# Layer 0 of a two-layer graph network: a row tile's normalisation, transposes and mask copies issued several units later

**Chip, cores, metric.** One core of one Trainium2 chip. The metric is the device time of one execution in microseconds (us); a kernel's figure is the median of its timed runs. Lower is better.

## The reference, cut to what matters

Two layers over 4096 nodes with 512 features. Layer 0 is a graph attention with four heads and a full 4096 x 4096 0/1 mask, then a residual and a normalisation; layer 1 is a masked attention with eight heads.

```python
support = (inputs @ weight).reshape(N, H, D).transpose(1, 0, 2)     # layer 0, H = 4, D = 128
logits = f1 + f2
w = jnp.where(logits >= 0, logits, SLOPE * logits)
masked = w * adjacency[None]
attn = jax.nn.softmax(jnp.where(masked != 0, masked, NEG), axis=-1) * (masked != 0)
out = jnp.einsum('hij,hjd->hid', attn, support)
out = out + bias + inputs @ proj_w + proj_b
x = _layernorm(x + out)                                             # input of layer 1
# ... layer 1: q, k, v, masked softmax, projection, residual, _layernorm
```

## The kernel before

The program order is the order on each engine: each engine takes its own instructions one after the other (in the prediction's timeline ScalarE's copy at 597.05 starts only after the normalise that waited 5.24 us), and the kernel's author decides by hand where each one stands. A small list named `Later` puts off a piece of work by a number of steps:

```python
class Later:
    def at(self, steps, fn): self.todo.append((self.n + steps, fn))
    def step(self):
        self.n += 1
        due = [fn for n, fn in self.todo if n <= self.n]
        ...
```

Layer 0's attention handles 8 row tiles (a group, W = 1024 rows) at a time, for each of four heads, over 32 column tiles. One (group, head, column tile) is a **unit**: eight matmuls into o_ps. Work of unit n+3 is prepared (`front`) before the matmuls of unit n are issued:

```python
            def front(w, h, j):                       # ... loads cut
                if j % 2 == 0:                        # ScalarE: two masks z, VectorE: az
                    z = wp.tile([P, 2, W], BF16, name="z")
                    ...
                p = wp.tile([P, W], F32, name="p", bufs=LA + 1)      # VectorE; LA = 3
                ...
            for n, (w, h, j) in enumerate(steps):
                if n + LA < len(steps):
                    front(*steps[n + LA])
                ...
                if w + 1 < NW and u % 3 == 0 and u // 3 < NT:        # u = h * NT + j
                    take = transpose_adj(w + 1, u // 3, ps)          # PE: masks of the next group
                for t in range(WT):
                    nc.tensor.matmul(o[t // BK][:, t % BK, :], ...)
                if take:
                    take()                            # ScalarE copies the transposed masks
                if j == NT - 1:
                    finish(w, h, o_t.pop((w, h)))
                later.step()
            later.flush()
```

When a group's last head is done, `finish` plans the **closing** of its eight row tiles, which then runs inside the first units of the next group (for the fourth group there is no next, and it runs alone):

```python
                for t in range(WT):
                    later.at(4 + t, lambda t=t: divide(t))               # ScalarE
                    if h == H0 - 1:
                        later.at(5 + t, lambda t=t: add_base(w, t))      # GpSimd's DMA adds the residual
                        later.at(8 + 3 * t, lambda t=t: close(w, t))

            def close(w, t):
                y = agg_t[w][:, t].rearrange("p h d -> p (h d)")
                mv, rs = moments(y)          # VectorE statistics, GpSimd: + EPS, power -0.5
                nb = small.tile([P, 1], F32, name="nb")                  # GpSimd, two more
                nc.gpsimd.tensor_tensor(nb, mv[:, 0:1], rs, op=ALU.mult)
                nc.gpsimd.tensor_scalar(nb, nb, -1.0, None, op0=ALU.mult)

                def normalise():             # ScalarE, then a store
                    nc.scalar.activation(y, y, AF.Identity, bias=nb, scale=rs)
                    nc.sync.dma_start(x1_d[i], y)
                later.at(2, normalise)
                later.at(4, lambda: turn(y, i))

            def turn(y, i):                  # PE: four transposes into the one bank x_ps
                p = ps.tile([P, KC, P], F32, name="x_ps", bufs=1)
                ...
                later.at(1, lambda: turned(p, i))

            def turned(p, i):                # ScalarE copies the bank out, then a store
                x1T = wp.tile([P, KC, P], F32, name="x1T")
                nc.scalar.activation(x1T, p, AF.Copy)
                nc.sync.dma_start(x1T_d[i // GT]..., x1T)
```

## Time and profile before

| | before |
|---|---|
| median of runs | 3967.98 us (3965.11 to 3968.51) |
| PE busy, whole span | 3799.8 us, 96% |
| layer 0's attention, first matmul to last | 315.84 to 1366.6 us |
| first matmul of layer 1 | 1408.96 us |

In the trace the engines are PE (matmuls), PEld (PE's weight loads), DVE (VectorE), ACT (ScalarE), POOL (GpSimd) and SP (SyncE). The page, the windows, the waits and a piece of timeline are read in the prediction below. One ruler is used all through this text. The mask transposes (at_ps) come every three units in the first three heads of a group, 32 per group. So the distance between two of them on PE's timeline is the time of a known number of units, and can be compared between kernels:

- **closing 1 and 2**: from mask transpose 0 of the second and third group to number 12 (36 units, holding the whole closing of the group before). With PE full this would be 12 x 5.86 + 8 x 0.49 = 74.2 us, from the spacing of mask transposes where PE is full and the time of a tile's x_ps transposes.
- **head 4**: from mask transpose 31 of the second group to the next group's first (35 units, nearly all without masks).
- **last stretch**: from mask transpose 31 of the third group to the last matmul (163 units, holding the third closing).
- **tail**: from the last matmul to layer 1's first. The last matmul's end is the start of the tail's first x_ps transpose minus the wait listed with it.

### The profile page before, as it was taken

What the parts mean: (1) busy time and instruction counts of PE and PEld (TensorE: products, weight loads), DVE (VectorE), ACT (ScalarE), POOL (GpSimd) and SP (SyncE); (2) the same over time, 40 slices, a digit from 0 to 9 for tenths busy, and PEclk for the clock granted to TensorE, in tenths of its full rate; (3) what the DMA queues carried; (4) which work ended last, traced back from release to release, by engine and by line L of the source; (5) the groups of instructions that cost most, each with busy time, mean ns of one, the idle gap of its engine ahead of it and who ended that gap; (6) DMA issues with size and microseconds to landing.
All of it is one profiled execution on the core that took longest, in us unless ns stands there. A gap on an engine that the chain in (4) does not pass through costs nothing. (4 is left out here: it accounts for less than half of the span.)

```text
span 3967.4 us, 51832 instructions
## 1 busy us (share of the span) xinstructions
PE 3799.8 (96%) x20490; PEld 1985.2 (50%) x20490; DVE 2532.6 (64%) x2432; ACT 1855.8 (47%) x2113; POOL 2046.3 (52%) x1211
## 2 busy tenths in 40 slices
PE   7988998999989889989999999999999999999998
PEld 3448998989989734433333333333333333333332
DVE  3447998988989801125666666666666666666665
ACT  1226767767656510024444444444444444444443
POOL 2320012021030100018888888888887888888886
PEclk9998999999999989999999999999999999999999
DMA  6885566656431143242222322322323223223211
GB/s 163 193 199 162 131 195 157 175 161 160 150 109 63 43 148 111 98 146 83 96 83 80 117 83 79 113 88 78 109 74 114 80 88 117 80 77 115 75 63 54
DMA packets 232429, 447.47 MB, mean 113 GB/s; under 512 B 21744, under 2 KB 136688, under 8 KB 225008
## 3 DMA queue, kind: packets, MB, share of 16 engines
q1 hardware_dynamic: 179264, 386.38, 29.4%
q0 software_dynamic: 42432, 51.39, 7.8%
q10 hardware_dynamic: 10480, 6.29, 0.5%
q8 instruction: 163, 2.67, 0.3%
q14 instruction: 90, 0.74, 0.1%
HBM read 372.51 MB, written 100.86 MB: 119 GB/s over the span
## 5 line engine op out<-in xcount | busy, mean ns | idle before, releaser
L959 POOL TENSOR_TENSOR q_sum<-q_sum,p 128x1024 f32<-128x1024 f32 x704 | 1659.0, 2356 | 332.6 <-DVE p L951 287.2
L951 DVE TENSOR_TENSOR p<-s_ps,adjT 128x1024 f32<-128x1024 f32 x896 | 1043.8, 1217 | 686.1 <-ACT s_ps L945 669.1
L945 ACT ACTIVATE s_ps<-s_ps 128x1024 f32<-128x1024 f32 x1024 | 971.1, 1009 | 1004.2 <-PE s_ps L936 1004.1
L796 PE MATMUL o_ps<-sup_t,p 128*128 128x129 f32 x8192 | 966.0, 279 | 42.4 <-DVE p L719 42.4
L936 PE MATMUL s_ps<-q_sb,k_sb 64*128 64x512 f32 x4096 | 981.6, 610 | 16.8 <-issue 10.2
L796 PEld LDWEIGHTS o_ps<-sup_t,p 128*128 128x128 f32 x8192 | 941.5, 194 | 52.2 <-issue 29.6
L969 PE MATMUL o_ps<-p,v_sb 128*64 128x512 f32 x4096 | 956.5, 601 | 0.0
L936 PEld LDWEIGHTS s_ps<-q_sb,k_sb 64*128 64x128 f32 x4096 | 367.6, 187 | 628.4 <-issue 388.4
L719 DVE SCALAR_TENSOR_TENSOR p<-fr_t,dj,az 128x1024 f32<-128x1024 f32 x512 | 635.5, 1280 | 27.7 <-DVE az L715 0.9
L712 ACT ACTIVATE z<-fr_t,f1s 128x1024 bf16<-128x1024 f32 x512 | 555.5, 1141 | 132.8 <-DVE az L715 106.3
L969 PEld LDWEIGHTS o_ps<-p,v_sb 128*64 128x64 f32 x4096 | 263.1, 136 | 649.7 <-issue 621.3
L715 DVE TENSOR_TENSOR az<-adjT,z 128x2048 bf16<-128x2048 bf16 x256 | 311.6, 1217 | 88.4 <-ACT z L712 88.2
L752 POOL DMA_DIRECT2D agg<-base_d x32 | 29.0, 1120 | 443.2 <-ACT agg L740 442.8
L538 POOL DMA_DIRECT2D arow<-in_adj_dram x32 | 30.7, 960 | 402.0 <-PE at_ps L553 402.0
L560 ACT ACTIVATE stage<-at_ps 128x1024 bf16<-128x1024 bf16 x128 | 130.7, 1021 | 206.5 <-PE at_ps L553 200.9
L951 DVE TENSOR_TENSOR p<-s_ps,md 128x1024 f32<-128x1024 f32 x128 | 150.4, 1216 | 94.7 <-ACT s_ps L945 93.4
L886 POOL DMA_DIRECT2D md<-adjT_d x8 | 6.6, 824 | 354.9 <-DMA v_d<-vg 354.6
L840 DVE COPY kg<-k_ps 128x512 f32<-128x512 f32 x32 | 22.1, 692 | 196.2 <-PE k_ps L837 190.1
L980 PE MATMUL sm_ps<-p,ones 128*32 128x512 f32 x1024 | 136.4, 605 | 0.0
L847 ACT ACTIVATE qg<-q_ps 128x512 f32<-128x512 f32 x32 | 19.1, 597 | 237.4 <-PE q_ps L844 237.4
L837 PE MATMUL k_ps<-xT,wk 128*128 128x512 f32 x256 | 118.1, 605 | 12.5 <-DMA xT<-x1T_d 12.5
L661 DVE TENSOR_TENSOR prod<-sup,uv 128x512 f32<-128x512 f32 x64 | 51.7, 807 | 117.6 <-ACT sup L657 117.6
(91 smaller groups left out, 2107.3 us busy)
## 6 DMA issues: line engine op xcount, KB each, us to landing
adjT<-adjT_d SPq DMA_DIRECT2D x64, 1024.0 KB, 7.1
k_sb<-k_d SPq DMA_DIRECT2D x128, 512.0 KB, 3.5
v_sb<-v_d SPq DMA_DIRECT2D x128, 512.0 KB, 3.6
sup_t<-sup_d SPq DMA_DIRECT2D x16, 2064.0 KB, 13.1
arow<-in_adj_dram POOLq DMA_DIRECT2D x32, 1024.0 KB, 12.5
adjT_d<-stage SPq DMA_DIRECT2D x64, 512.0 KB, 5.7
fr_t<-fr_d SPq DMA_DIRECT2D x16, 1024.0 KB, 8.9
sup_d<-sup SPq DMA_DIRECT2D x32, 258.0 KB, 10.9
```

The source lines that it names most:

```text
L560: nc.scalar.activation(s[:, j % 2, :], p.rearrange("p t r -> p (t r)"), AF.Copy)
L712: nc.scalar.activation(z[:, k, :], fr[:, 0, :], AF.Abs, bias=f1s[:, j + k, h:h + 1], scale=BIG)
L715: nc.vector.tensor_tensor(az, adjT[w, j // CJ][:, j % CJ:j % CJ + 2, :], z, op=ALU.min)
L719: nc.vector.scalar_tensor_tensor(p, fr[:, 1, :], dj[:, j, h:h + 1], az_t[w, h, j // 2][:, j % 2, :], op0=ALU.max, op1=ALU.mult)
L796: nc.tensor.matmul(o[t // BK][:, t % BK, :], p[:, t * P:(t + 1) * P], sup_t[w, h][:, j, :], start=(j == 0 and t % BK == 0), stop=(j == NT ...
L837: nc.tensor.matmul(k_ps, w3["wk"][:, c, m * P:(m + 1) * P], xT[:, c, :], start=(c == 0), stop=(c == KC - 1))
L936: nc.tensor.matmul(s[:, e, :], k[r, a:a + P], qt[g, m][r, :], start=True, stop=True)
L945: nc.scalar.activation(s, s, AF.Exp)
L951: nc.vector.tensor_tensor(p, s, mask.to_broadcast([P, HP, G]), op=ALU.mult)
L959: nc.gpsimd.tensor_tensor(q_sum[g, m], q_sum[g, m], p, op=ALU.add)
L969: nc.tensor.matmul(o[r, :], v[:, j % CH, r], p[:, e, :], start=(j == 0), stop=(j == NT - 1))
L980: nc.tensor.matmul(sm_t[g, m][r:r + QD, :], ones[:, 0:QD], pt[g, m, j - 1 + n][:, e, :], start=(j == 3), stop=(j + 6 >= BY_PE))
```

## The change

The intent: put distance between the instruction that needs a result and the one that makes it, so that an engine that takes its work in order doesn't stand in front of a result that is still on its way.

```diff
-                        later.at(8 + 3 * t, lambda t=t: close(w, t))
+                        later.at(8 + 2 * t, lambda t=t: close(w, t))
...
-                later.at(2, normalise)
-                later.at(4, lambda: turn(y, i))
+                later.at(6, normalise)
+                later.at(9, lambda: turn(y, i))
...
-                later.at(1, lambda: turned(p, i))
+                later.at(2, lambda: turned(p, i))
...
                 if take:
-                    take()
+                    later.at(2, take)
```

The cut rest gathers the statistics and the four GpSimd operations into one helper, `normal_factors`, also used by the last layer, with the same operations in the same order. `take` is called outside a step, so `at(2, take)` means the end of the next unit.

More of the change, by code (lines that the diff above doesn't have):

```diff
@@ L508, in on_all_partitions, with normal_factors @@
         return bass.AP(tensor=src.tensor, offset=src.offset, ap=[[0, P], [1, n]])
-    def moments(y):
+    def normal_factors(y):
         st = small.tile([P, 6], F32, name="bn_st")
@@ L518, in moments @@
         nc.gpsimd.tensor_tensor(rs, ve, minus_half, op=ALU.pow)
-        return mv, rs
-    def layernorm(dst, y):
-        mv, rs = moments(y)
-        nc.vector.tensor_scalar(dst, y, mv[:, 0:1], rs, op0=ALU.subtract, op1=ALU.mult)
+        nb = small.tile([P, 1], F32, name="bn_nb")
+        nc.gpsimd.tensor_tensor(nb, mv[:, 0:1], rs, op=ALU.mult)
+        nc.gpsimd.tensor_scalar(nb, nb, -1.0, None, op0=ALU.mult)
+        return rs, nb
     with tc.tile_pool(name="l0", bufs=1) as l0, \
@@ L757, in close @@
                 y = agg_t[w][:, t].rearrange("p h d -> p (h d)")
-                mv, rs = moments(y)
-                nb = small.tile([P, 1], F32, name="nb")
-                nc.gpsimd.tensor_tensor(nb, mv[:, 0:1], rs, op=ALU.mult)
-                nc.gpsimd.tensor_scalar(nb, nb, -1.0, None, op0=ALU.mult)
+                rs, nb = normal_factors(y)
                 def normalise():
@@ L1016, in close1 @@
                 nc.vector.tensor_tensor(y, y, s, op=ALU.add)
-                mv, rs = moments(y)
-                nb = small.tile([P, 1], F32, name="nb")
-                nc.gpsimd.tensor_tensor(nb, mv[:, 0:1], rs, op=ALU.mult)
-                nc.gpsimd.tensor_scalar(nb, nb, -1.0, None, op0=ALU.mult)
+                rs, nb = normal_factors(y)
                 def normalise():
```

## The prediction

> **What bounds the kernel now.** I read the page first, then busy time by windows, then the waits of one window, then its timeline.
>
> ```profile
> PE 3799.8 (96%) x20490; PEld 1985.2 (50%) x20490; DVE 2532.6 (64%) x2432; ACT 1855.8 (47%) x2113; POOL 2046.3 (52%) x1211
> PE   7988998999989889989999999999999999999998
> ```
>
> PE is the engine to feed, and 96% leaves 168 us without a matmul in the whole kernel. The 9s with 8s between them are layer 0's attention, slices 3 to 13. It runs four groups of eight row tiles; a group takes 128 units (four heads of 32), a unit being eight matmuls. The group's normalisation and transposes ("closing") run inside the first units of the next group. Windows (us from the start, PE, PEld, DVE, ACT, POOL busy, granted clock, DMA share, GB/s):
>
> ```profile
> 570.00:660.00 90.00, 76.02 (x670) 73.62 (x669) 69.08 (x75) 59.36 (x73) 35.28 (x43) 0.96 0.61 138
> 660.00:840.00 180.00, 180.00 (x1674) 178.95 (x1673) 172.37 (x160) 125.36 (x137) 5.29 (x6) 1.00 0.59 178
> 840.00:930.00 90.00, 74.75 (x667) 72.00 (x667) 68.92 (x74) 59.38 (x73) 34.99 (x42) 0.98 0.62 141
> 930.00:1097.00 167.00, 167.00 (x1548) 165.89 (x1547) 159.51 (x144) 117.96 (x129) 2.63 (x3) 1.00 0.52 160
> 1097.00:1185.00 88.00, 72.91 (x599) 70.66 (x599) 72.23 (x76) 45.59 (x56) 33.02 (x40) 0.96 0.38 100
> 1366.00:1409.00 43.00, 9.59 (x39) 6.22 (x37) 7.67 (x20) 12.77 (x24) 20.60 (x44) 0.55 0.87 230
> ```
>
> Between closings PE is full at clock 1.00. In the three closings it loses 14 to 15 us each and the clock dips. The last window is the fourth closing, with no matmuls left to hide it. Waits from 570 to 650 (us, times, longest):
>
> ```profile
> ACT agg L764 <- POOL nb L761: 28.3, 5, 6.0
> DVE az L715 <- ACT z L712: 14.1, 4, 3.6
> PE x_ps L772 <- ACT x1T L777: 10.1, 4, 3.1
> PE o_ps L796 <- DVE p L719: 2.9, 3, 1.1
> ```
>
> These are one chain read from the top: POOL delivers the factors late, ACT stands before its normalise, and behind it in ACT's order stand the copy that frees PE's only transpose bank and the masks z that DVE needs. The timeline (start, duration, engine, operation):
>
> ```profile
> 591.14 0.18 DVE L514 BATCH_NORM_AGGREGATE bn_mv<-bn_st 128x2 f32<-128x6 f32 x1
> ...
> 591.42 1.15 POOL L516 TENSOR_SCALAR bn_ve<-bn_mv 128x1 f32<-128x1 f32 x1 [3.75 <-DVE bn_mv L514]
> 592.66 1.41 POOL L518 TENSOR_TENSOR bn_rs<-bn_ve,minus_half 128x1 f32<-128x1 f32 x1
> 594.15 0.92 POOL L760 TENSOR_TENSOR nb<-bn_mv,bn_rs 128x1 f32<-128x1 f32 x1
> 595.15 1.15 POOL L761 TENSOR_SCALAR nb<-nb 128x1 f32<-128x1 f32 x1
> ...
> 596.33 0.81 ACT L764 ACTIVATE agg<-agg,nb,bn_rs 128x512 f32<-128x512 f32 x1 [5.24 <-POOL nb L761]
> 597.05 0.57 ACT L777 ACTIVATE x1T<-x_ps 128x512 f32<-128x512 f32 x1
> 597.68 0.66 PE L772 MATMUL x_ps<-ident,agg 128*128 128x128 f32 x4 [3.08 <-ACT x1T L777]
> 598.17 2.88 PE L796 MATMUL o_ps<-sup_t,p 128*128 128x129 f32 x16
> ```
>
> The wait ends 5.2 us after the statistics. It arises because tile t's copy and tile t+1's normalise fall into the same unit (13+3t), the normalise first. The matmuls after it take 2.88 us instead of the usual 1.95: the clock from 599.0 to 601.7 was 0.50.
>
> **What the Trainium skill says.** "GPSIMD Engine Reference", Specifications: its SBUF interfaces are shared with VectorE and contend with DVE instructions in a two-port mode or with two SBUF inputs. The trace agrees: the four POOL operations take 1.15, 1.41, 0.92 and 1.15 us beside a running DVE and 0.22, 0.57, 0.19 and 0.24 at 599.1 when DVE stands. "TensorE: Matmul & The Clock Gate", Part 1, says an idle window of about 3.4 us brings half clock; here 3.08 us (with 1.14 shortly before) did. "Perfetto Trace Analysis", Identifying the Most-Contended Engine: consistent bubbles can mean too few buffers; with one x_ps bank the bubbles are consistent, but the bank is held by a late copy, so order may cure it. "DMA: Bandwidth & Descriptors", Anatomy of one DMA, gives about 2 us fixed cost; the store of x1T lands after a median of 6.2 us, so load decides here.
>
> **The change part by part.** Closings start every 2 units instead of 3. The normalise comes 6 units after the statistics (was 2), the transposes after 9 (was 4), the copy out of x_ps 2 units after them (was 1); a mask transpose is copied at the end of the next unit (was the same). The number of matmuls, activations, bytes and POOL operations is the same; the last layer's close only gets a shared helper, with its order kept. So nothing is saved in work; only waits can go.
>
> (a) What is to be had, first two closings. Mask transposes start every 5.86 us (three units) where PE is full. Eight such groups, 24 units, with eight sets of x_ps transposes at 0.49 us of issue, should take 8 x 5.86 + 8 x 0.49 = 50.8 us. From the mask transpose at 580.99 to that at 650.88 they take 69.9: 19.1 lost, 14.0 as listed waits and the rest as slow clock. Second closing, 850.69 to 926.43, nine groups: 75.7 against 56.7, also 19.1.
> (b) Third closing. No mask transposes; DVE sets the pace at 3.72 us for two units (az 1.23, two p 2.48). A tile's statistics add about 0.82 to 0.85. From 1111.47 to 1185.21 there are 28 units: 14 x 3.72 + 8 x 0.85 = 58.9 us expected, 73.7 taken: 14.8 lost.
> Sum 19.1 + 19.1 + 14.8 = 53.0 us.
>
> (c) Does the new order fit? In units: the copy of tile t stands at 19+2t, its neighbours' normalises at 18+2t and 20+2t, the next transposes at 19+2t. The normalise before it, of tile t+2, had its statistics at 12+2t, six units or some 13 us before. Per two units PE needs 2 x 1.805 + 0.30 (masks) + 0.49 = 4.4 us; DVE 3.72 + 0.85 = 4.57; ACT start to start 2.09 (two z) + 0.72 + 0.48 + 0.60 (masks) = 3.9. DVE falls back 0.17 x 8 = 1.4 us in a closing, and its four p buffers allow a lead of three units, over 5 us. POOL needs 4 to 4.9 us per tile beside DVE, and the base DMAs (0.92 each) and an adjacency load lie between the early tiles, so it lags by some 4 to 5 us: factors about 9 us after the statistics, four units. ACT runs up to four units ahead, so it may still wait there, but then keeps about two units before anything is needed. The next transposes wait for a copy that has two units (4 us) to take 0.6. I charge 1 us per closing: gain 50.
>
> (d) The tail after the last matmul has no matmuls to delay behind, so later issue there is pure order. POOL has eight closes at 1.5 us and eight base DMAs at 0.92, ending near 1389 in both orders. But the first copy now stands after the third normalise (about 1381, was 1378.4), and x1T has two buffers, so each copy waits for a store two tiles back, at the 4.5 to 8.3 us these stores took. Worked through, the last copy ends 0 to 4 us later than now (1400.4). I charge 2 us.
>
> Net 50 - 2 = 48 us, 1.2%: 3968 - 48 = 3920.
>
> **The rivals.**
> 1. POOL takes the place of the removed wait. For: 4.9 us per tile against closings every 4.57, and its queue holds the base DMAs too. Against: it is short of rate only by little and over eight tiles; two units of slack remain. If its lag doubled, half the 53 us would stay: 3943.
> 2. Copies wait for the x1T stores. For: in the first two closings these stores landed after 9.1 and 9.3 us (median), and two tiles now pass in about 9.0 us, so each pair may slip by about 1 us. Against: three slips of 1 us stay under the two units of slack; in the third closing stores landed in 2.8. If the slack were used up: some 10 us lost, 3930.
> 3. The order is neutral because DVE is the bound anyway. In the stretches between closings PE and DVE are almost level, so DVE caps the gain; but DVE itself was kept idle 14.1 us by ACT in the first closing. That it caps all: 3955 at the worst, and unlikely.
> 4. More gain than counted, by a shorter tail: its 43 us are mostly POOL and DMA latency, which the change doesn't shorten. A few us at best: 3912.
>
> **Range and chances.** The mechanism is listed wait by wait, and nothing in work is added, so the sign is fairly sure. Two per cent is 79 us, more than all the waits of the three closings and half of the tail together. Runs of before lie within 3.4 us. Predicted 3921 (one more us for rivals), range 3911 to 3939; faster by over 2%: 0.02, within 2%: 0.97, slower: 0.01.
>
> **What would show each step.** Right: in the closings' windows PE over 98% busy at clock 1.00; PE's waits for x1T gone before the tail (23 us or more now) and its waits for p down to the first 29.4; mask transposes near 50.8 us for eight groups; ACT still waiting for nb in short pieces, without PE waiting after. The tail 43 to 47 us. Wrong: PE still waiting for x1T with ACT behind nb (rival 1) or behind x1T stores (rival 2); PE waiting for p or at_ps in the closings, which would mean that ACT's lead was miscounted; or a tail longer than 50 us.

## The result

| | before | changed |
|---|---|---|
| median | 3968.12 us (3965.11 to 3968.51, 4 runs) | 3913.89 us (3910.23 to 3914.50, 4 runs) |
| ratio | | 0.9863, 95% interval 0.9846 to 0.9880 |
| closing 1 | 93.5 | 76.4 |
| closing 2 | 93.5 | 78.6 |
| head 4 | 64.5 | 63.0 |
| last stretch | 328.3 | 311.8 |
| tail | 42.3 | 42.2 |
| layer 1's first matmul at | 1408.96 | 1356.10 |

A ratio is the mean time of one kernel's runs over that of the other's in the same rounds, so it is not quite the ratio of the medians. By the criterion of 2% the two count as the same; the interval shows a real gain of 1.4%, 54 us.

The ruler itself, on PE's timeline (start, duration, engine and line, operation, count, wait in brackets). Before:

```profile
580.99 0.61 PE L553 MATMUL at_ps<-ident_b,arow 128*128 128x128 bf16 x8
588.82 0.61 PE L553 MATMUL at_ps<-ident_b,arow 128*128 128x128 bf16 x8 [0.54 <-ACT stage L560]
600.85 1.06 PE L553 MATMUL at_ps<-ident_b,arow 128*128 128x128 bf16 x8
607.90 0.61 PE L553 MATMUL at_ps<-ident_b,arow 128*128 128x128 bf16 x8
```

The changed kernel, the same three distances:

```profile
579.13 0.61 PE L553 MATMUL at_ps<-ident_b,arow 128*128 128x128 bf16 x8
585.23 0.61 PE L553 MATMUL at_ps<-ident_b,arow 128*128 128x128 bf16 x8
...
592.49 0.61 PE L553 MATMUL at_ps<-ident_b,arow 128*128 128x128 bf16 x8
599.25 0.61 PE L553 MATMUL at_ps<-ident_b,arow 128*128 128x128 bf16 x8
```

Where three units took 7.8, 12.0 and 7.1 us they now take 6.1, 7.3 and 6.8. The windows of the changed kernel (columns as in the prediction):

```profile
570.00:630.00 60.00, 58.82 (x550) 57.83 (x550) 58.14 (x60) 51.02 (x61) 36.16 (x41) 1.00 0.79 184
820.00:880.00 60.00, 57.18 (x529) 55.54 (x528) 57.73 (x60) 48.26 (x59) 35.96 (x41) 1.00 0.77 177
1060.00:1140.00 80.00, 75.38 (x651) 73.08 (x650) 76.92 (x87) 53.16 (x63) 35.93 (x40) 1.00 0.53 154
```

The closings are shorter, and the clock stays at 1.00 in all three, where it was 0.96 to 0.98. PE is not quite full in the second and third: in the third DVE is the busiest (76.9 of 80). Waits of the changed kernel from 570 to 650 (us, times, longest):

```profile
ACT agg L761 <- POOL bn_nb L522: 3.9, 4, 1.9
ACT x1T L774 <- DMA x1T_d<-x1T: 3.2, 2, 1.8
...
PE o_ps L793 <- DVE p L719: 1.2, 3, 0.7
```

ScalarE still stands before a normalise now and then, but 3.9 us instead of 28.3, and PE doesn't wait for the copy at all there. A new small wait has come: the copy waits for an older store (x1T_d). The same two waits over all of layer 0's attention and the tail, 330 to 1440, before:

```profile
ACT agg L764 <- POOL nb L761: 103.5, 19, 8.4
PE x_ps L772 <- ACT x1T L777: 43.9, 19, 3.8
```

The changed kernel:

```profile
ACT agg L761 <- POOL bn_nb L522: 28.8, 20, 5.4
PE x_ps L769 <- ACT x1T L774: 16.4, 9, 6.6
```

Of PE's waits for the copy, 13.4 us lie in the tail before and 15.0 in the changed kernel.

**Where the 52.9 us to layer 1's first matmul came from.** Start of the attention 0.2, first group 1.7, closing 1 17.2, the rest of the second group 1.8 (head 4 1.5), closing 2 14.9, the rest of the third group's heads with masks 0.6, last stretch 16.5, tail 0.1: together 53.0, the difference being rounding. From there to the end the two traces differ by another 2.3 us in a layer whose order is the same; over all twelve traces that stretch scatters between 2555.5 and 2559.9 us without pattern, so it is taken as noise.

### The profile page after: what moved, and what is told of

Its sections match the earlier page's. It is cut to its first block, busy times and chain, and to the rows that moved or that the text cites. A ratio compares the mean times of both kernels' runs of the same rounds, so it can differ in the third digit from the quotient of the medians.

```text
span 3912.2 us, 51842 instructions
## 1 busy us (share of the span) xinstructions
PE 3780.8 (97%) x20490; PEld 1971.1 (50%) x20490; DVE 2536.0 (65%) x2432; ACT 1858.0 (47%) x2113; POOL 2055.2 (53%) x1211
## 5 line engine op out<-in xcount | busy, mean ns | idle before, releaser
L933 PE MATMUL s_ps<-q_sb,k_sb 64*128 64x512 f32 x4096 | 980.9, 610 | 16.4 <-issue 10.1
L793 PE MATMUL o_ps<-sup_t,p 128*128 128x129 f32 x8192 | 951.6, 277 | 37.9 <-DVE p L719 37.8
L793 PEld LDWEIGHTS o_ps<-sup_t,p 128*128 128x128 f32 x8192 | 929.7, 192 | 46.1 <-issue 29.4
L715 DVE TENSOR_TENSOR az<-adjT,z 128x2048 bf16<-128x2048 bf16 x256 | 311.7, 1218 | 26.6 <-ACT z L712 26.5
```

The source lines that it names most:

```text
L715: nc.vector.tensor_tensor(az, adjT[w, j // CJ][:, j % CJ:j % CJ + 2, :], z, op=ALU.min)
L793: nc.tensor.matmul(o[t // BK][:, t % BK, :], p[:, t * P:(t + 1) * P], sup_t[w, h][:, j, :], start=(j == 0 and t % BK == 0), stop=(j == NT ...
L933: nc.tensor.matmul(s[:, e, :], k[r, a:a + P], qt[g, m][r, :], start=True, stop=True)
```

## The experiments

All times beside the kernel before on the same chip, whose median was 3967.81 to 3968.37 us. Each timed run has four or five executions, and all passed the comparison with the reference. Ruler in us:

| run | median | ratio | closing 1 | closing 2 | head 4 | last stretch | tail |
|---|---|---|---|---|---|---|---|
| before | 3968.1 | | 93.5 | 93.5 | 64.5 | 328.3 | 42.3 |
| changed | 3913.9 | 0.9863 | 76.4 | 78.6 | 63.0 | 311.8 | 42.2 |
| close_only | 3923.1 | 0.9885 | 77.6 | 78.3 | 64.5 | 313.2 | 43.9 |
| take_only | 3959.3 | 0.9982 | 92.2 | 92.5 | 63.0 | 326.8 | 40.1 |
| dve_factors | 3918.6 | 0.9878 | 77.7 | 77.7 | 64.5 | 315.4 | 38.0 |
| swap_only | 3945.5 | 0.9946 | 84.3 | 86.0 | 64.5 | 323.0 | 40.6 |
| spacing_only | 3954.5 | 0.9965 | 90.2 | 90.3 | 64.6 | 323.4 | 41.4 |
| pool6 | 3933.0 | 0.9911 | 82.4 | 82.0 | 63.0 | 316.2 | 42.3 |
| after_dve | 3918.6 | 0.9873 | 79.8 | 79.4 | 63.0 | 314.2 | 38.4 |
| stores4 | 3911.0 | 0.9853 | 76.3 | 76.8 | 63.0 | 311.6 | 38.8 |
| head_only | 3913.2 | 0.9864 | 76.4 | 76.8 | 63.0 | 311.8 | 40.4 |
| early_load | 3903.3 | 0.9836 | 76.3 | 76.8 | 63.0 | 311.7 | 32.2 |

Each row of the ruler is one traced execution. Stretches with the same program order show how far such a row can be trusted: closing 2 is 78.6 in changed and 76.8 in head_only, whose edit comes after it, and the tail is 42.3 in before and 40.1 in take_only, 42.2 in changed and 43.9 in close_only. So differences of 2 us in closing 2 or in the tail are not read as effects.

The theory: the gain is ScalarE no longer standing before late factors with urgent work behind it. The rivals: the spacing, the transpose bank, the mask copies.

### close_only and take_only: which part does what

```diff
 # close_only: changed kernel            # take_only: kernel before
-                    later.at(2, take)   -                    take()
+                    take()              +                    later.at(2, take)
```

> The changed kernel with one part undone: the copy of a transposed mask is issued at once again, in its own unit; the closing stays late. Theory of two parts: the closings give about 45 us and the late mask copies about 1.8 us in each of the three groups with masks, outside the closings (VectorE fills its lead and spends it in the head without masks). So 3919 to 3922 us, about 6 us above the changed kernel; PE in the third to fourth head of a group back at the pace of before, the closings nearly as short as in the changed kernel. Rival, that the late mask copies also carry the closings (ScalarE stands at a mask copy and so loses what it has in hand): 3930 to 3945, with PE waits for p or at_ps in the closings.

> The kernel before with one part alone: the copy of a transposed mask is issued at the end of the next unit; the closings as before. Theory of two parts: 6 us less than before, 3960 to 3964, with closings as long as before (about 19 us lost in each of the first two) and VectorE waiting for free p buffers between closings instead of for z. Rival: the mask copies matter in the closings as well: 3950 or less.

Measured 3923.1 (1 us over the expectation) and 3959.3 (1 us under it). The closings are nearly the same with and without the late mask copies (77.6 and 78.3 against 76.4 and 78.6), so the rival falls. Head 4 shows the second part by itself, and sharply: 63.0 in every kernel with late mask copies, 64.5 or 64.6 in every kernel without. The waits from 330 to 500, between closings, say why. Before:

```profile
ACT stage L560 <- PE at_ps L553: 47.0, 28, 2.8
DVE az L715 <- ACT z L712: 5.2, 11, 0.7
```

The changed kernel:

```profile
ACT stage L560 <- PE at_ps L553: 44.9, 26, 2.8
...
DVE p L719 <- PE o_ps L793: 2.6, 9, 0.5
```

ScalarE stands at the mask copy in both. Before, it stood there so early in its order that VectorE then waited for masks z behind it (5.2 us) and never filled its four p buffers; in the changed kernel VectorE waits for PE to free a p buffer instead, that is, its lead is full. That the late mask copies do this is shown by the two runs: from 330 to 500 take_only has the same wait for p buffers (2.6 us, 9 times) and none for z, close_only the wait for z (6.0 us, 11 times) and none for p buffers. With the lead full it pays in head 4, where without mask transposes VectorE (3.72 us for two units) is slower than PE (3.61): PE lives on the lead for a while and gains 1.5 us. The effect is small, but it comes in each group.

### dve_factors: the factors early, the order old

```diff
-                mv, rs = moments(y)                      # GpSimd: + EPS, power
-                nc.gpsimd.tensor_tensor(nb, mv[:, 0:1], rs, op=ALU.mult)
-                nc.gpsimd.tensor_scalar(nb, nb, -1.0, None, op0=ALU.mult)
+                (statistics as before)
+                nc.vector.tensor_scalar(rs, mv[:, 1:2], -0.31763646, 1.289470, op0=ALU.mult, op1=ALU.add)
+                nc.vector.scalar_tensor_tensor(nb, mv[:, 0:1], -1.0, rs, op0=ALU.mult, op1=ALU.mult)
```

> The kernel before, in its old order, but the normalisation's two factors are worked out by two small VectorE operations (the power replaced by a straight line through the middle of the variances, so the result is wrong by a few per cent of some rows on purpose) and no longer by four GpSimd operations. Theory that the cause is the lateness of the factors at ScalarE's normalise (4 to 5 us after the statistics): 3925 to 3935 us with the old order, ScalarE's waits of 5 us before the normalise gone and PE's waits for the copy out of x_ps mostly gone outside the tail; the tail shorter by 3 to 8 us as well. Rival, that the single transpose bank and the place of its copy in the order are the cause whatever the factors take: 3955 or more, with PE's waits for the copy staying at 20 us.

Measured 3918.6, even better than expected: the old order with early factors has closings of 77.7 us, about as short as the new order with late ones. So the lateness of the factors is the cause, and the single bank and the place of its copy do no harm when the factors are there. One more rival, that GpSimd's operations slow VectorE beside them, falls with the same traces: in closing 1 the operations that make p and az take 1.28 and 1.22 us on average before, and 1.28 and 1.22 here. One part of the expectation missed. Waits of this run from 330 to 1440:

```profile
ACT agg L770 <- DVE nb L766: 49.0, 26, 4.7
...
PE x_ps L778 <- ACT x1T L783: 15.2, 7, 8.8
```

ScalarE still waits 49 us before normalises (103.5 before), with 4.7 the longest. It runs ahead of the others and stands wherever its lead ends; here that alone cost nothing, since PE waits for no normalise outside the tail. PE's 15.2 us behind the copy are all in the tail (seven waits, the seven tiles after the first).

### swap_only: one digit

```diff
-                later.at(2, normalise)
+                later.at(3, normalise)
```

> The kernel before with one digit changed: the normalise comes 3 units after the statistics instead of 2, which puts the copy out of x_ps ahead of the next tile's normalise in ScalarE's order. Theory that the copy standing behind a waiting normalise makes PE wait: PE's waits for that copy fall from 24 us outside the tail to under 8, but ScalarE still stands before some normalises and the masks z behind it are late, so 3940 to 3955 us. Rival, that only the length of ScalarE's stand counts: the waits move to p, and the time stays at 3963 or more.

Measured 3945.5, as the first theory expected, but its number for the wait of before was wrong (30.5 us outside the tail, not 24: 43.9 in all less 13.4 in the tail). The waits from 330 to 1440:

```profile
ACT agg L764 <- POOL nb L761: 68.4, 20, 6.4
PE x_ps L772 <- ACT agg L764: 45.0, 23, 7.8
```

PE no longer waits for the copy at all. It waits for the normalise itself: 23.2 us outside the tail, since its transposes come one unit behind. So this digit took 40% of the gain, and the remaining wait took another name. The digit does two things: it puts the copy ahead of the next normalise, and it gives the factors one unit more (ScalarE's waits for them fall from 103.5 to 68.4 us). What each is worth by itself is not shown. Distance is needed on both sides of the normalise.

### spacing_only, and a version that can't be built

```diff
-                        later.at(8 + 3 * t, lambda t=t: close(w, t))
+                        later.at(8 + 2 * t, lambda t=t: close(w, t))
```

> The kernel before with one part alone: row tiles start their closing every 2 units instead of 3, with the old short delays (normalise after 2, transposes after 4, copy after 1). Theory that delay, not spacing, brings the gain: ScalarE still stands 4 to 5 us before the normalises, GpSimd has less time between tiles and the stands come closer together; 3955 to 3985 us, PE's waits in the closings not under 12 us each. Rival, that a shorter closing is a gain by itself: 3950 or less.

Measured 3954.5, just under the theory's range: the spacing by itself brings a quarter of the gain, 3 us in each of the first two closings (90.2 and 90.3) and 5 in the last stretch, with PE waits of 10.5 us per closing on average, a little under the 12 that I expected. The rest of the gain needs the delay.

The reverse, the new delays with the old spacing of 3, doesn't build: the compiler's scheduler finds a deadlock. Counted in units, the last tile's transposes, at 8 + 3 x 7 + 9 = 38, need the bank that the copy of the tile before frees, at 8 + 3 x 6 + 9 + 2 = 37. But ahead of that copy on ScalarE stands the next head's first `divide`, at 32 + 4 = 36, and it waits for the agg tile that those transposes still read. With a spacing of 2 that copy comes at 31. Builds alone, not timed, fit this count: at the old spacing, delays of 6, 7 and 2 or of 6, 8 and 1 build (that copy at 35), and 6, 8 and 2 or 6, 9 and 1 deadlock (at 36). So a run of delay without the closer spacing was possible, with 6, 7 and 2, and was not made: what delay gives by itself is not measured.

### pool6: how much is in hand

```diff
                 rs, nb = normal_factors(y)
+                for _ in range(2):
+                    nc.gpsimd.tensor_scalar(nb, nb, 1.0, None, op0=ALU.mult)
```

> The changed kernel with two more GpSimd operations on a tile's factor (times one, the result stays right): six instead of four. Theory that six units of delay leave only a few us in hand against GpSimd's rate beside VectorE (about 1.2 us an operation, 4.57 us between tiles): GpSimd falls behind by 2 to 3 us more per tile, the last tiles' normalises wait, and each of the three closings loses 4 to 12 us; with some 5 us more in the tail 3930 to 3950 us. Rival, that GpSimd has ample room in the new order: only the tail's 4 to 6 us, 3917 to 3921.

Measured 3933.0, inside the theory's range. The closings lengthen by 6.0, 3.4 and 4.4 us (the last from the last stretch); the tail doesn't lengthen (42.3), against the expectation. (The traced execution is the fastest of its four, so its rows hold 15.5 of the 19 us between the medians.) Two more operations of GpSimd, 0.21 us each in the tail, where it is alone, undo a third of the gain: six units of delay leave little in hand.

### after_dve: what is left in the closings

The edit of dve_factors on the changed kernel.

> The changed kernel with the factors from two VectorE operations (power replaced by a straight line, a few per cent wrong on purpose). Theory that what the changed kernel still loses in the closings (about 8 us in three) is mostly VectorE's own rate and the copies' stores, since ScalarE's waits for factors no longer reach PE: no shorter closings, VectorE gets 0.35 us more per tile, the tail 3 to 8 us shorter as GpSimd's eight chains go: 3906 to 3914 us. Rival, that late factors still cost in the closings: they fall to the pace of full PE, 3903 or less.

Both expectations missed: 3918.6, 4.7 us slower than the changed kernel. The tail shortened by 3.8 us as expected, but closing 1 is 3.4 longer than in the changed kernel, closing 2 0.8 and the last stretch 2.4. The waits from 330 to 1440 of this run:

```profile
PE o_ps L802 <- DVE p L719: 15.8, 25, 1.4
PE x_ps L778 <- ACT x1T L783: 15.1, 7, 8.3
```

The changed kernel's PE waits for p only 8.5 us from 330 to 1440. The two operations take 0.15 and 0.16 us, 2.5 us per closing, and most of that came out as time. This fits VectorE as the bound inside a closing in the new order: the work that was moved to it is paid for. GpSimd's slow chain, hidden by the delay, is the better place. And early factors and late issue don't add up: both together take as long as early factors alone (dve_factors, 3918.6). The second closing of the changed kernel (78.6) also holds a wait for stores, which not every execution has (next section).

### stores4, head_only, early_load: the second closing and the tail

```diff
 # stores4 and early_load
-                x1T = wp.tile([P, KC, P], F32, name="x1T")
+                x1T = wp.tile([P, KC, P], F32, name="x1T", bufs=4)
 # head_only and early_load: layer 1's first load_xT(0) now stands ahead of the weights
-                nc.sync.dma_start(xTs[g], x1T_d[g])
+                (nc.sync if g else nc.gpsimd).dma_start(xTs[g], x1T_d[g])
-            for name, src, eng in (("wk", wks, nc.scalar), ("wq", wqs, nc.gpsimd),
+            for name, src, eng in (("wk", wks, nc.gpsimd), ("wq", wqs, nc.gpsimd),
```

> The changed kernel with four buffers in place of two for the transposed tile that is stored (x1T). Theory that in the second closing and in the tail the copy out of x_ps waits for a store two tiles back (2.9 us and 7 us of ScalarE waits in the changed kernel's trace): PE's waits for that copy inside the second closing (1.4 us) gone, the tail 3 to 6 us shorter, 3906 to 3911 us. Rival, that the tail is POOL's chain and the first load of the next layer anyway: 3912 to 3915.

> The changed kernel with four x1T buffers and the next layer's first input tile and its key weights loaded by GpSimd's queue, ahead of the query weights, and no longer behind the stores of the last closing on SyncE's queue and behind the last copy on ScalarE's. Theory that after the last closing PE waits about 10 us for a load that was issued only because SyncE's queue came free: that wait falls to 0 to 3 us, and with the shorter tail 3896 to 3904 us. Rival, that the load can't be earlier (memory of the last stage, or DMA engines full): 3906 or more.

> The changed kernel with only the earlier loads of the next layer (first input tile and key weights on GpSimd's queue), the two x1T buffers kept. If the earlier loads and the four buffers each take a piece of the tail: 3905 to 3909 us. If the loads alone do it: 3902 to 3904. If the loads need the shorter chain of copies ahead of them: 3911 or more.

stores4: 3911.0, within its range, but 2.9 us is no clear gain (its executions lie between 3909.3 and 3912.2, the changed kernel's between 3910.2 and 3914.5). The tail falls from 42.2 to 38.8. Closing 2 falls from 78.6 to 76.8, but head_only, with two buffers and the same closings, has 76.8 too: ScalarE waits 3.3 us for stores there, and PE not at all for the copy. So those 1.8 us are not shown to be the buffers' doing. early_load: 3903.3, within its range, with a tail of 32.2: the fastest kernel, 1.6% under the kernel before (ratio 0.9836). head_only, however, gains nothing that can be told from noise (3913.2, from 3910.4 to 3919.1). The waits from 330 to 1440, in head_only:

```profile
PE x_ps L769 <- ACT x1T L774: 23.3, 7, 6.5
ACT x1T L774 <- DMA x1T_d<-x1T: 18.8, 6, 6.4
```

In the changed kernel the second of these was 13.1 us; in early_load this wait is no longer there. The tail's end shows where it went. The changed kernel:

```profile
1344.54 1.12 PE L769 MATMUL x_ps<-ident,agg 128*128 128x128 f32 x4 [3.04 <-ACT x1T L774]
1356.10 5.44 PE L834 MATMUL k_ps<-xT,wk 128*128 128x512 f32 x8 [10.45 <-DMA xT<-x1T_d]
```

head_only:

```profile
1353.22 1.11 PE L769 MATMUL x_ps<-ident,agg 128*128 128x128 f32 x4 [5.89 <-ACT x1T L774]
1355.07 6.36 PE L834 MATMUL k_ps<-xT,wk 128*128 128x512 f32 x8 [0.74 <-ACT x1T L774]
```

early_load:

```profile
1340.89 1.11 PE L769 MATMUL x_ps<-ident,agg 128*128 128x128 f32 x4 [0.73 <-ACT x1T L774]
1345.71 5.08 PE L834 MATMUL k_ps<-xT,wk 128*128 128x512 f32 x8 [3.71 <-issue]
```

The earlier load takes PE's wait for xT from 10.5 us to nothing, but with two buffers the last copies wait longer for stores, and PE's last transposes come 8.7 us later (7.9 when both are counted from the last matmul). The wait moved by one step. With four buffers no copy waits for a store, and both gains stay. That the stores land later, and because the weights now share the DMA engines with them, is likely, and not shown.

## Why the prediction was right

Predicted 3921 (3911 to 3939), measured 3913.9: inside the range, 7 us under the middle. The mechanism that it named, late factors in front of urgent work, is the one that the runs show. By its steps:

- **(a) and (b), 53 us to be had in the closings.** Right in size. They gave 17.2 and 14.9 us, and the third about 15.0 (16.5 of the last stretch less the 1.5 us that head 4 gains): 47.1. Eight groups of mask transposes take 52.8 us in the first closing, where 50.8 was the sign asked for. The split in (a) was off: half clock held for 2 x 3.41 us in that stretch, which costs at most 3.4 us of the 5.1 that it was given; the other 1.7 stay unexplained. And the stores' medians, 9.1, 9.3 and 2.8 us (2.4 on reading again), rest on three landings each, the only ones of eight that the trace tells.
- **(c), 1 us lost per closing.** Too little. Some 6 us stayed: closing 1 is 2.2 us and closing 2 4.4 us over the 74.2 of a full PE. In the second, PE waits 1.4 us for a copy held by stores (rival 2), which head_only doesn't have; what is left moves with VectorE's load (after_dve), so rival 3 is probably the bound that remains. The closing's VectorE row, 4.57 us for two units against PE's 4.4, was the right row to look at.
- **(c) also took VectorE's lead of three units as given, and charged the late mask copies nothing.** This is the step that failed. In the kernel before the lead was not full (its waits for z between closings, 5.2 us from 330 to 500), and filling it gave about 5.5 us outside the closings: 1.7 in the first group, 1.8 in the second, 0.6 in the third, and some 1.5 in the last stretch.
- **(d), the tail 2 us longer.** It stayed (42.3 and 42.2), just under the 43 to 47 asked for. The first copy came 3.0 us later after the last matmul, as foreseen, but ScalarE's waits for stores in the tail fell from 9.3 to 7.0 us and the last copy ended 0.2 us earlier. With 2 us of scatter between tails of the same order, one trace each can't say more.
- **Rival 1** (GpSimd as the new bound) was near: ScalarE waited for factors, without PE behind it, and pool6 shows that two operations more would have made it true. **Rival 2** was true in a small way: in closing 2 of some executions, and in the tail. **Rival 4** was not seen in the change itself; early_load shows that the tail could be shortened, by other means.
- **The signs asked for.** The clock at 1.00 in the closings came true. PE's waits for the copy before the tail fell from 30.5 to 1.4 us. PE over 98% busy came true only in the first closing (58.8 of 60), and its waits for p kept 8.5 us beside the first one (13.0 before).

The sum: 47 us in the closings against 50, about 5.5 not foreseen, 0 instead of -2 in the tail, one us that I took off for rivals, and some 2 us of layer 1's scatter make some 8 us; the two traced executions differ by 55.2 us where the medians differ by 54.2, which leaves the 7 between 3921 and 3914. That the total came so near is in part luck: the closings gave 3 us less than charged, and 5.5 came from a step that was not counted at all. The main cause, late factors in front of urgent work, is shown by dve_factors, where the factors come early in the old order, and by the change itself; swap_only agrees.

## What to carry to other kernels

When an engine takes its work in order and stands before a late result, look at what stands behind that instruction in the same order; the cost is there, and either an earlier result or a later issue removes it. A later issue costs nothing in work, but it needs room until the buffer's next use, and it only helps by as much as the slack that it makes: count the slack in units for each engine, and find which one is the next bound before moving work onto it. After each move look for the same wait under another name: here it went from the copy to the normalise in one run, and from a load to a store in another.

## What the Trainium skill lacked or had wrong

- "GPSIMD Engine Reference", Specifications, names the shared SBUF interfaces without a cost. That the loser of a shared port is held for the other engine's whole instruction does stand in the skill ("SBUF — State Buffer", Terms); what it costs a chain of small operations doesn't. Here four operations on one column took 1.15, 1.41, 0.92 and 1.15 us beside a running VectorE, and 0.22, 0.57, 0.19 and 0.24 without, so the chain took 4.9 us instead of 1.5; three of the four ended within 0.1 us after the VectorE operation beside them.
- "TensorE: Matmul & The Clock Gate", Part 1, gives an idle window of about 3.4 us for half clock. Here a wait of 2.28 us (with 0.74 and 0.36 us in the 8 us before) was enough: it ended at 1130.6, from 1131.5 to 1134.9 the granted clock was 0.50, and 32 matmuls took 5.48 us instead of about 3.8.
- "DMA: Bandwidth & Descriptors", Anatomy of one DMA: its fit for GpSimd's path, 2.0 us plus bytes over 436 GB/s, would give 2.6 us, by this estimate, for the 256 KB of an x1T store (128 x 512 x 4 bytes). The stores are on SyncE's queue. There the three landings that the trace tells took 2.4 to 2.6 us in the changed kernel's third closing, but 10.1, 7.9 and 2.5 in its second, at a DMA share of 0.77; the page has no time to landing for transfers beside others.
- "Perfetto Trace Analysis", Optimization Strategy, says that consistent bubbles can mean too few buffers. Here they came from the order of issue and late factors, with the buffer unchanged (dve_factors); no page was found that speaks of what stands behind a waiting instruction.
